# One set of sorted tiles in a fused attention and mixture-of-experts layer, with the last router begun inside the last projection

## The chip, the cores and the metric

The kernel runs on one core of a Trainium2 chip. The core has TensorE (PE; its weight loads are PEld), VectorE (DVE), ScalarE (ACT), GpSimd (POOL) and SyncE (SP), each with a queue of its own that is worked off in order, and 16 DMA engines that carry what SP and POOL issue. The metric is the device time of one execution in microseconds. All arithmetic is in float32.

## The reference

Two batches of 1024 tokens, 256 wide. Modulated layer norm, attention with 16 query heads of 128 and one shared key/value head, an output projection, a second layer norm and a gated residual; then a second modulated norm and a mixture of 8 experts of which each token takes two:

```python
h = _layernorm(x) * (1 + ca) + sa
x = x + ga * attention(h)            # q, k normalised; softmax; @ Wout; layernorm
h = _layernorm(x) * (1 + cb) + sb
x = x + gb * moe(h)

def _moe(x):
    logits = xf @ router_w.T
    topk_vals, topk_idx = jax.lax.top_k(logits, K)        # K = 2
    topk_w = jax.nn.softmax(topk_vals, axis=-1)
    order = jnp.argsort(exp_id)
    x_sorted = xf[order // K]
    y1 = ragged_dot(x_sorted, w1, counts)                 # 256 -> 2 * 176
    y_act = silu(gate) * up
    y2 = ragged_dot(y_act, w2, counts)                    # 176 -> 256
    # back to the tokens' order, times exp_w, the sum of a token's two rows
```

`counts`, how many of the 4096 (token, expert) pairs each expert has, is known only at run time.

## The kernel before

Tokens are held as 16 row tiles of 128 (`NT`), in four blocks of four (`NBLK`, `QT`). The kernel has two stages.

**Attention** (lines 228 to 865) goes block by block. In a block, `attention` walks over 16 heads times 8 key tiles: `s` (L478), exp on ACT (L482), `o` (L493) and the sums on DVE (L498). Other work is hung into these steps by hand with `at(h, j, f)`. `project` (L541) multiplies by Wout, 16 heads for each of the four row tiles (`pr`, L547), and copies each result to `o` with ACT. `Settle` (L570) does what follows for a block: statistics of the output (`of_outputs`, with the rsqrt on POOL at L177 and L178), `residual`, statistics again (`norms`), then for each row tile `logits`: the modulated row on DVE, two transposes (`tp`, L620), a copy on ACT (`rT`), the router's matmuls (`lg`, L625). `weights` finds the two experts of every token (`chosen`) and their weights, with an exp on ACT (L656). `count` numbers the pairs of each expert (two matmuls, then 18 small DVE instructions). For blocks 0 to 2 all this is hung into the attention of the next block. For the last block there is no next block: its router is run in the second stage.

**Experts** (lines 867 to 1066). Sorted tiles of 128 pairs, all of one expert, lie in DRAM (`sorted_x`). There are two separate sets (`SETS`): the pairs of blocks 0 to 2 in set 0, those of the last block in set 1. Each set must have room for any distribution over 8 experts, each with its own unfinished tile: `tiles_for` gives 31 and 15, 46 in all. `bases` turns counts into places (`place_i`) and gives each tile its expert (`at_w1`, `at_w2`). Rows are put in their places by indirect DMAs from POOL (`scatter`, L742), one for each row tile and each of a token's two choices: 24 for set 0, inside the last block's attention, and 8 for set 1. `choose_second` on POOL swaps weight and destination in the rows between the first choices and the second, so it waits for the first choices' scatters.

A loop of 50 steps pipelines the 46 tiles: step `m` does `turn(m)` (two transposes, `xp`, L913), `up(m-1)` (`su`, L928, Silu on ACT L936, product on DVE L938), `gates` and `turn_back(m-3)` (`ap`, L944), and `down(m-4)` (`sy`, L959). DVE evicts with weight and gate into `ysb` (L967, four buffers), and an indirect DMA on POOL puts the rows into `results` (L970), at the place that the row itself carries. Loads of sorted tiles on SP run seven tiles ahead (`PRE`).

Into the same loop are hung, for the last block: `residual` at steps 0 to 3, `norms` at 4, `logits` at 5 to 8, `weights` at 9, `count` at 10, `bases` at 11, and one scatter a step at 12 to 19. Tiles of set 1 begin at step 31.

From step 36 on, `fetch` (L997) loads a row tile's results, three tiles in two steps, as soon as all of set 0 is written, and two steps later `combine` (L1009, L1010) adds the two results and x on DVE and stores (L1011). The last four row tiles are fetched after the loop, when set 1 is complete.

Each engine's queue keeps the planned order: a planner works from priorities in program order and a model of costs; `issue_after` puts an instruction behind a given one on its engine.

Of the kernel before, what the change touches and what calls it, by code (L numbers as in the profile page):

```python
# [28 lines left out]

# [26 lines left out]
def tile_adaln_attention_moe(  # L56
# [36 lines left out]
    def tiles_for(n):  # L93

        return (TOP * n * P + E * (P - 1)) // P

    NM = [tiles_for(t1 - t0) for t0, t1 in SETS]
    MOST = max(t1 - t0 for t0, t1 in SETS)
# [20 lines left out]
    at_w1 = [keep.tile([P, n], I32, name=f"at_w1_{i}") for i, n in enumerate(NM)]  # L119
    at_w2 = [keep.tile([P, n], I32, name=f"at_w2_{i}") for i, n in enumerate(NM)]  # L120

# [38 lines left out]
    counts = const.tile([P, NM[0]], FP, name="counts")  # L160
    minus_half = const.tile([P, QT], FP, name="minus_half")
    nc.vector.memset(minus_half, -0.5)
    rank = const.tile([P, E], FP, name="rank")
# [18 lines left out]
    def statistics(pool, rows, n, name):  # L182
# [11 lines left out]
    sorted_x = [dram.tile([n * P, ROW], FP, name=f"sorted_x{i}") for i, n in enumerate(NM)]  # L194
    results = [
        dram.tile([(TOP * (t1 - t0) + NM[i]) * P, D], FP, name=f"results{i}")
        for i, (t0, t1) in enumerate(SETS)
    ]

    class Scattered:  # L200
# [5 lines left out]

        def add(self, ins):
            ins = ins.ins
            tc.declare_no_dep(ins, group=self.name, reason="each writes rows of its own")
            tc.add_to_no_dep_group(self.name, ins)  # L210
            self.all.append(ins)

        def read(self, ins):
            for s in self.all:
                tc.add_manual_dep(
                    ins.ins,
                    s.name,
                    mybir.DependencyInfo(mybir.DependencyClass.Sync, mybir.DependencyReason.DATA),
                    reason="reads what they wrote",
                )  # L220

    into_x = [Scattered(f"into_x{i}") for i in range(len(SETS))]
    into_results = [Scattered(f"into_results{i}") for i in range(len(SETS))]
# [4 lines left out]
    with ExitStack() as attn:  # L228
# [58 lines left out]
        def tables():  # L287


            with tc.issue_after(latest["pool"]), tc.issue_after(latest["vector"]):  # L290
                for m in range(NM[0]):
                    nc.vector.memset(counts[:, m : m + 1], float(m))
                for e in range(E):
                    nc.vector.memset(rank[:, e : e + 1], float(E - e))
                for t0, t1 in SETS:
                    to = second_to[:, t0:t1]
                    nc.gpsimd.iota(to, [[TOP * P, t1 - t0]], base=0, channel_multiplier=TOP)
                    nc.vector.tensor_copy(rows[:, t0:t1, TO].bitcast(I32), to)
                    nc.vector.tensor_scalar(to, to, 1, None, ALU.add)
                for b in range(B):  # L300
                    nc.vector.memset(rows[:, b * TPB : (b + 1) * TPB, BATCH:], float(b))

        def clear_sorted():
# [3 lines left out]
            for i, (n, to) in enumerate(zip(NM, sorted_x)):  # L307
                by_tile = to.rearrange("(m p) d -> p m d", p=P)
                nc.sync.dma_start(out=by_tile, in_=zero.unsqueeze(1).to_broadcast([P, n, ROW]))
                nobody = work.tile([P, n, 1], I32, tag="z", name=f"nobody_{i}")  # L310
                nc.gpsimd.iota(
                    nobody, [[P, n]], base=TOP * (SETS[i][1] - SETS[i][0]) * P, channel_multiplier=1
                )
                with nc.allow_non_contiguous_dma(reason="one number of each row"):
                    nc.sync.dma_start(out=by_tile[:, :, TO : TO + 1].bitcast(I32), in_=nobody)
# [225 lines left out]
        def project(blk, q, last):  # L541

            o = work.tile([P, QT, D], FP, tag="proj", name=f"proj_{blk}", bufs=1)
# [17 lines left out]
            for i in range(2):  # L561
                heads(ps[i], i, first, HEADS)
                nc.scalar.copy(o[:, i, :], ps[i])
            for i in range(2, QT):
                ps = ps_m.tile([P, D], FP, tag="mm", name=f"pr_{blk}_{i}")
                heads(ps, i, 0, HEADS)
                nc.scalar.copy(o[:, i, :], ps)
            return o

        class Settle:  # L570


            def __init__(self, blk, o):
                self.blk, self.o = blk, o
# [6 lines left out]
            def of_outputs(self):  # L581
                o = self.o
                self.mv, self.rs = statistics(
                    small, [o[:, i, :] for i in range(QT)], QT, f"o{self.blk}"
                )

            def residual(self, i0, i1):
# [4 lines left out]
                for i in range(i0, i1):  # L592
                    nc.vector.tensor_scalar(
                        o[:, i, :], o[:, i, :], self.mv[:, i, 0:1], self.rs[:, i : i + 1],
                        ALU.subtract, ALU.mult,
# [5 lines left out]
            def norms(self):  # L601
                blk = self.blk
                self.mv, self.rs = statistics(
                    self.small, [xs[:, blk * QT + i, :] for i in range(QT)], QT, f"x{blk}"
                )

            def logits(self, i):
# [3 lines left out]
                row = rows[:, t, :D]  # L611
                nc.vector.scalar_tensor_tensor(
                    row, xs[:, t, :], self.mv[:, i, 0:1], one_cb, ALU.subtract, ALU.mult
                )
                nc.vector.scalar_tensor_tensor(
                    row, row, self.rs[:, i : i + 1], sb, ALU.mult, ALU.add
                )
# [3 lines left out]
                rT = self.wide.tile([P, DC, P], FP, tag="h", name=f"rT_{t}")  # L621
                nc.scalar.copy(rT, tp)
                lg = self.psum.tile([P, E], FP, tag=self.tag, name=f"lg_{t}")
# [6 lines left out]
            def weights(self):  # L630
# [25 lines left out]
                nc.scalar.activation(e2, e2, AF.Exp)  # L656
# [5 lines left out]
        filled = [keep.tile([P, E], FP, name=f"filled_{i}") for i in range(len(SETS))]  # L662
        for f in filled:
            nc.vector.memset(f, 0.0)
        end = keep.tile([P, E], FP, name="end")

        filled_in = filled

        def count(blk, filled, work, psum, tag):
# [22 lines left out]
        def bases(i, work):  # L692

            t0, t1 = SETS[i]
            filled = filled_in[i]
            over = work.tile([P, E, MOST], FP, tag="z", name=f"over_{i}")
            nc.vector.tensor_scalar(
                over, counts[:, :MOST].unsqueeze(1).to_broadcast([P, E, MOST]), float(P), None, ALU.mult
            )
            nc.vector.tensor_tensor(  # L700
                over, filled.unsqueeze(2).to_broadcast([P, E, MOST]), over, ALU.is_gt
            )
            nc.vector.tensor_reduce(filled, over, AX.X, ALU.add)
            nc.vector.tensor_copy(end[:, 0:1], filled[:, 0:1])
            for e in range(1, E):
                nc.vector.tensor_tensor(
                    end[:, e : e + 1], end[:, e - 1 : e], filled[:, e : e + 1], ALU.add
                )
            nc.vector.tensor_tensor(filled, end, filled, ALU.subtract)
            nc.vector.tensor_scalar(filled, filled, float(P), None, ALU.mult)  # L710
            n = (t1 - t0) * TOP
            base = work.tile([P, n, E], FP, tag="h", name=f"base_{i}")
            nc.vector.tensor_tensor(
                base,
# [396 lines left out]
```

## Time and profile before

| | |
|---|---|
| time, median of 3 runs | 1354.47 us (1352.80 to 1355.57) |
| the profiled execution | 1353.75 us |
| its span, first to last instruction | 1352.0 us |
| granted TensorE clock, mean | 0.991 |
| TensorE busy | 98% of the span |
| DVE, ACT, POOL busy | 51%, 36%, 17% |
| last attention matmul to last projection matmul | 1186 to 1215.9 us |
| sorted tiles on TensorE | 1216.3 to 1337.9 us |

A group's line on the page reads: line, engine and operation, tiles written and read, number of instructions | busy us, mean ns of one | idle time of the engine just before, and what ended it. A timeline's line reads: start, length, engine, line, operation, tiles, number; in brackets the idle time before it and what released it. A row of the table by stretches reads: from:to, length, then busy us and instructions of PE, PEld, DVE, ACT and POOL, the granted clock, the DMA engines' busy share, and GB/s.

### The profile page before, as it was taken

The numbers are of one execution on the slowest core, as the hardware profiler recorded it, in microseconds if no ns is written. First come the engines' busy times: TensorE is split into PE (matmuls) and PEld (weight loads), VectorE is DVE, ScalarE is ACT, GpSimd is POOL, SyncE is SP. The second block draws the span as 40 slices with busy tenths as digits, with TensorE's granted clock in tenths as the row PEclk, the third lists the DMA queues.
The fourth block names the chain that finished last, engine by engine and source line by source line (L and its number), as shares of the span: only waits on it lengthen the run. The fifth ranks groups of instructions, "written<-read, shape, count | busy, mean of one in ns | idle before, by whom it ended". The sixth has DMA issues, their size and how long they took to land.

```text
span 1352.0 us, 12731 instructions
## 1 busy us (share of the span) xinstructions
PE 1322.1 (98%) x4024; PEld 686.6 (51%) x4024; DVE 685.4 (51%) x1380; ACT 489.4 (36%) x954; POOL 229.1 (17%) x325
## 2 busy tenths in 40 slices
PE   7899999999999999999999999999999999999995
PEld 3444444446644444447444444457444444476774
DVE  6356655544535554542636353544546544437645
ACT  2433344442243433330343333321333333304442
POOL 4200212110100111000100000001000224003633
PEclk9899999999999999999999999999999999999998
DMA  7000000000003410000001200100001013013435
GB/s 245 1 0 19 13 15 18 1 31 32 1 1 121 93 32 0 31 1 32 0 1 32 86 32 0 32 1 32 1 0 32 26 54 103 31 32 119 135 123 194
DMA packets 46322, 59.18 MB, mean 44 GB/s; under 512 B 10672, under 2 KB 32432, under 8 KB 46256
## 3 DMA queue, kind: packets, MB, share of 16 engines
q1 hardware_dynamic: 42512, 48.08, 11.6%
q0 software_dynamic: 3744, 10.29, 2.1%
q8 instruction: 33, 0.54, 0.2%
q14 instruction: 33, 0.27, 0.1%
HBM read 39.69 MB, written 18.66 MB: 43 GB/s over the span
## 4 chain that ended last, share of the span: by engine, by line
PE 93%; DVE 2%; DMA 2%; POOL 2%; issue 1%; ACT 0%; SPq 0%; POOLq 0%; DVEq 0%; ACTq 0%
PE s L478 32%; PE o L493 32%; PE pr L547 8%; PE q L441 8%; PE su L928 3%; PE sy L959 2%; PE qp L455 2%; PE den L507 1%; DMA out_dram<-res 1%; PE kv L384 1%; PE ap L944 1%; PE xp L913 1%; POOL rn_q L178 0%; PE lg L625 0%; DMA wmod_sb<-in_wmod_dram 0%
## 5 line engine op out<-in xcount | busy, mean ns | idle before, releaser
L478 PE MATMUL s<-qT,kT 128*128 128x512 f32 x1024 | 525.5, 595 | 0.1
L493 PE MATMUL o<-p,vs 128*128 128x512 f32 x1024 | 522.7, 593 | 0.0
L482 ACT ACTIVATE p<-s 128x512 f32<-128x512 f32 x512 | 305.6, 597 | 502.4 <-PE s L478 497.3
L498 DVE TENSOR_TENSOR sum<-sum,p 128x512 f32<-128x512 f32 x384 | 264.5, 689 | 180.2 <-ACT p L482 175.5
L493 PEld LDWEIGHTS o<-p,vs 128*128 128x128 f32 x1024 | 193.5, 190 | 233.2 <-issue 232.1
L478 PEld LDWEIGHTS s<-qT,kT 128*128 128x128 f32 x1024 | 187.4, 191 | 206.0 <-issue 204.1
L177 POOL TENSOR_SCALAR rn_q<-rn_q 128x4 f32<-128x4 f32 x64 | 14.0, 219 | 721.1 <-DVE rn_q L344 706.0
L441 PE MATMUL q<-wq_sb,rows 128*128 128x512 f32 x256 | 121.0, 596 | 0.0
L547 PE MATMUL pr<-wout_sb,qT 128*128 128x256 f32 x512 | 112.7, 381 | 0.0
L547 PEld LDWEIGHTS pr<-wout_sb,qT 128*128 128x128 f32 x512 | 96.7, 190 | 18.8 <-issue 4.3
L498 DVE TENSOR_TENSOR sum<-p,p 128x512 f32<-128x512 f32 x64 | 44.2, 691 | 113.4 <-ACT p L482 113.3
L344 DVE TENSOR_REDUCE rn_q<-sq_q 128x4 f32<-128x512 f32 x64 | 43.8, 684 | 84.0 <-ACT sq_q L343 83.9
L178 POOL TENSOR_TENSOR rn_q<-rn_q,minus_half 128x4 f32<-128x4 f32 x64 | 83.3, 1302 | 5.3
L441 PEld LDWEIGHTS q<-wq_sb,rows 128*128 128x128 f32 x256 | 49.1, 192 | 60.5 <-issue 50.5
L347 DVE TENSOR_TENSOR vn_q<-q,rn_q 128x512 f32<-128x512 f32 x64 | 44.2, 690 | 58.2 <-POOL rn_q L178 58.2
L343 ACT ACTIVATE sq_q<-q 128x512 f32<-128x512 f32 x64 | 38.2, 597 | 75.1 <-PE q L441 70.8
L523 DVE TENSOR_TENSOR qT<-qT,wide 128x512 f32<-128x512 f32 x64 | 42.2, 690 | 44.5 <-DMA wide<-spread 44.2
L515 DVE RECIPROCAL rden<-den 128x512 f32<-128x512 f32 x16 | 53.7, 3358 | 20.0 <-PE den L507 20.0
L928 PE MATMUL su<-w_sb,xT 128*128 x184 | 62.9, 462 | 0.2
L970 POOL DMA_INDIRECT results<-ysb,x x46 | 46.4, 1009 | 54.2 <-DVE ysb L967 37.9
L455 PEld LDWEIGHTS qp<-ident,vn_q 128*128 128x128 f32 x256 | 32.3, 143 | 37.3 <-issue 31.2
L959 PE MATMUL sy<-w2s,sactT 128*128 x184 | 47.2, 380 | 0.0
(160 smaller groups left out, 763.4 us busy)
## 6 DMA issues: line engine op xcount, KB each, us to landing
wide<-spread SPq DMA_DIRECT2D x64, 256.0 KB
x<-sorted_x SPq DMA_DIRECT2D x46, 130.0 KB
y<-results SPq DMA_DIRECT2D x16, 256.0 KB
sorted_x<-zero SPq DMA_DIRECT2D x1, 4030.0 KB
w_sb<-in_w_dram SPq DMA_DIRECT2D x2, 1408.0 KB
wout_sb<-in_wout_dram SPq DMA_DIRECT2D x1, 2048.0 KB
out_dram<-res SPq DMA_DIRECT2D x16, 128.0 KB
sorted_x<-zero SPq DMA_DIRECT2D x1, 1950.0 KB
```

What stands on the lines that cost most here:

```text
L178: latest["pool"] = nc.gpsimd.tensor_tensor(out, out, minus_half[:, : out.shape[1]], ALU.pow).ins
L441: nc.tensor.matmul(q.rearrange("p h d -> p (h d)"), hT[:, self.blk * QT + i, c, :], wq_sb[:, c, ts(g, QB)], start=(c == 0), stop=(c == DC ...
L455: nc.tensor.transpose(tp[:, j, :], qn[:, j, :], ident)
L478: nc.tensor.matmul(s, kT[:, ts(b * NJ + j, P)], q.head(h), start=True, stop=True)
L482: nc.scalar.activation(p, s, AF.Exp)
L493: nc.tensor.matmul(outs[h], vs[:, b * NJ + j, :], p, start=(j == 0), stop=(j == NJ - 1))
L498: latest["vector"] = nc.vector.tensor_tensor(sums[h], first, p, ALU.add).ins
L515: nc.vector.reciprocal(rden, den)
L547: nc.tensor.matmul(ps, q.head(h)[:, ts(i, P)], wout_sb[:, h, :], start=(h == 0), stop=(h == HEADS - 1),)
L928: nc.tensor.matmul(u, self.xT[:, c, :], w1_flat[:, c * I2 :][:, bass.ds(at, I2)], start=(c == 0), stop=(c == DC - 1),)
L959: nc.tensor.matmul(y, self.actT[:, c, :], w2_flat[:, c * D :][:, bass.ds(at, D)], start=(c == 0), stop=(c == 1),)
L970: ins = nc.gpsimd.indirect_dma_start(out=results[self.i], out_offset=bass.IndirectOffsetOnAxis(ap=self.x[:, TO : TO + 1].bitcast(I32), axi ...
```

## The change

There is one set. The first three blocks fill `full[e]` whole tiles of each expert `e`, at least 17 together (`FULL`); these come first. Then comes one tile for each expert, its unfinished one (8; with the whole ones at most 32, `ONES`), and the last block's pairs fill these up before they open further tiles; 39 tiles are room for everything (`ALL`). `place_first` gives the first three blocks' pairs their places, `place_second` those of the last block, and both share `places`, `experts`, `tiles_of` and `summed`. `at_w1`, `at_w2`, `sorted_x` and `results` are one tile or tensor each instead of two. Tiles 0 to 16 are loaded after the first 24 scatters, all others after all 32.

`Settle` works on ranges of row tiles: `all_norms(i0, i1)` does both statistics and the residual, `turn` is split from `logits`. In the last block `project` takes steps in `between`: the norms of row tiles 0 to 2, and the router of tiles 0 and 1, are issued among the last projection's matmuls. The rest comes earlier in the expert loop (`late`). The last block's eight scatters go out as two groups of four at steps 9 and 10. The exp of the weights is a power on POOL. The tables of numbers are made by an iota. `ysb` has five buffers. Fetches of the first twelve row tiles begin when tiles 0 to 31 are written, two a step.

```diff
-    NM = [tiles_for(t1 - t0) for t0, t1 in SETS]
+    FULL = -((E * (P - 1) - TOP * SETS[0][1] * P) // P)
+    ONES = TOP * SETS[0][1] + E
+    ALL = (TOP * NT * P + E * (P - 1)) // P
+    PARTS = 3
...
-                for m in range(NM[0]):
-                    nc.vector.memset(counts[:, m : m + 1], float(m))
+                nc.gpsimd.iota(at_w1, [[1, ALL]], base=0, channel_multiplier=0)
+                nc.vector.tensor_copy(counts, at_w1)
...
             for i in range(2, QT):
                 ps = ps_m.tile([P, D], FP, tag="mm", name=f"pr_{blk}_{i}")
-                heads(ps, i, 0, HEADS)
-                nc.scalar.copy(o[:, i, :], ps)
+                for g in range(NG):
+                    heads(ps, i, g * HG, (g + 1) * HG)
+                    if g == NG - 1:
+                        nc.scalar.copy(o[:, i, :], ps)
+                    done(i, g)
...
-                nc.scalar.activation(e2, e2, AF.Exp)
+                nc.gpsimd.tensor_tensor(e2, euler, e2, ALU.pow)
...
+        def place_second(work):
+            more = end[:, 2]
+            tiles_of(limit, work, ALU.is_gt, 0, NT)
+            nc.vector.tensor_scalar(full, full, 1.0, None, ALU.add)
+            nc.vector.tensor_tensor(limit, limit, full, ALU.subtract)
+            nc.vector.tensor_scalar(limit, limit, 0.0, None, ALU.max)
+            summed(more, limit)
+            nc.vector.tensor_tensor(
+                more, more, end[:, 1, E - 1 : E].to_broadcast([P, E]), ALU.add
+            )
+            nc.vector.tensor_tensor(below, end[:, 1], full, ALU.subtract)
+            nc.vector.tensor_tensor(above, more, limit, ALU.subtract)
+            nc.vector.tensor_tensor(above, above, end[:, 1], ALU.subtract)
+            nc.vector.tensor_scalar(limit, full, float(P), None, ALU.mult)
+            for table in (below, above):
+                in_rows(table)
+            places(1, work)
+            experts(FULL, ALL, PARTS, work, "past")
...
+                between = {
+                    (1, NG - 1): [lambda: settle.all_norms(0, 2)],
+                    (2, NG - 1): [lambda: settle.all_norms(2, 3)],
+                    (3, 1): [lambda: settle.turn(0)],
+                    (3, 2): [lambda: settle.logits(0), lambda: settle.turn(1)],
+                    (3, 3): [lambda: settle.logits(1)],
+                }
...
-                load = nc.sync.dma_start(out=self.x, in_=sorted_x[i][ts(m, P), :])
-                into_x[i].read(load)
+                load = nc.sync.dma_start(out=self.x, in_=sorted_x[ts(m, P), :])
+                into_x.read(load, TOP * (SETS[0][1] if m < FULL else NT))
...
-                ysb = mg.tile([P, D], FP, tag="ysb", name=f"ysb_{m}", bufs=4)
+                ysb = mg.tile([P, D], FP, tag="ysb", name=f"ysb_{m}", bufs=5)
...
+        late = {
+            0: [lambda: settle.all_norms(QT - 1, QT)],
+            1: [lambda: settle.turn(QT - 2)],
+            2: [lambda: settle.logits(QT - 2)],
+            5: [lambda: settle.turn(QT - 1)],
+            6: [lambda: settle.logits(QT - 1), settle.weights],
+            8: [lambda: count(NBLK - 1, mg, ps_t, "t"), lambda: place_second(mg)],
+        }
+        SCATTERS = 9
+        for m in range(ALL + LAG):
+            there = ALL if m >= SCATTERS + TOP else FULL
+            while len(tiles) < min(m + 1 + PRE, there):
+                tiles.append(Sorted(len(tiles)))
+            for f in late.get(m, ()):
+                f()
...
+            if SCATTERS <= m < SCATTERS + TOP:
+                k = m - SCATTERS
                 with tc.issue_after(tiles[m - LAG].scattered):
-                    k, t = n // QT, SETS[1][0] + n % QT
-                    if k and t == SETS[1][0]:
+                    if k:
                         choose_second(*SETS[1])
-                    scatter(place_i[:, t, k : k + 1], 1, t)
-
-            n = (m - (NM[0] + LAG)) * 3 // 2
-            for t in range(have, min(n, SETS[0][1])):
+                    for t in range(*SETS[1]):
+                        scatter(place_i[:, t, k : k + 1], t)
+
+            n = (m - (ONES + LAG - 1)) * 2
+            for t in range(have, max(have, min(n, SETS[0][1]))):
```

## The prediction

> **What bounds the kernel now.** I read the page first: shares of the span, the chain that ended last, the costliest groups.
>
> ```profile
> PE 1322.1 (98%) x4024; PEld 686.6 (51%) x4024; DVE 685.4 (51%) x1380; ACT 489.4 (36%) x954; POOL 229.1 (17%) x325
> L928 PE MATMUL su<-w_sb,xT 128*128 x184 | 62.9, 462 | 0.2
> L959 PE MATMUL sy<-w2s,sactT 128*128 x184 | 47.2, 380 | 0.0
> ```
>
> TensorE has work for 98% of the span. su and sy each have 184 matmuls, 4 for each of 46 sorted tiles. The change touches the end of this stretch, so next came the chain in order of time there.
>
> ```profile
> 1257.13 0.86 PE sy L959 x4
> 1258.21 1.19 PE su L928 x4
> 1259.62 0.86 PE sy L959 x4
> ...
> 1304.41 0.87 PE sy L959 x4
> ```
>
> From one sy to the next is 2.49 us: that is one sorted tile, and TensorE sets it. Then the timeline of TensorE, of DVE, of POOL, and of the last 10 us. Columns: start, length, engine and line, what ended the idle time before.
>
> ```profile
> 1216.32 0.88 PE L913 MATMUL xp<-ident,x 128*128 128x128 f32 x6 [0.46 <-ACT proj L567]
> 1222.47 0.44 PE L944 MATMUL ap<-ident,sact 128*128 128x128 f32 x2 [1.17 <-DVE sact L938]
> 1228.40 0.41 PE L620 MATMUL tp<-ident,rows 128*128 128x128 f32 x2 [0.29 <-DVE rows L615]
> 1259.46 1.03 PE L959 MATMUL sy<-w2s,sactT 128*128 x4
> ...
> 1240.76 0.17 DVE L628 COPY ls<-lg 128x8 f32<-128x8 f32 x1 [0.34 <-PE lg L625]
> 1246.05 0.16 DVE L685 TENSOR_TENSOR own<-count,filled 128x8 f32<-128x8 f32 x1
> 1250.42 0.21 DVE L688 TENSOR_REDUCE place<-own 128x8 f32<-128x64 f32 x1
> 1254.15 0.16 DVE L721 TENSOR_TENSOR place_i<-place,first 128x8 int32<-128x8 f32 x1
> ...
> 1262.15 0.96 POOL L742 DMA_INDIRECT sorted_x<-rows,place_i  x1 [0.30 <-issue]
> 1265.41 0.19 POOL L761 COPY rows<-share 128x4 f32<-128x4 f32 x1 [1.03 <-DMA sorted_x<-rows,place_i]
> 1266.13 1.23 POOL L742 DMA_INDIRECT sorted_x<-rows,place_i  x1 [0.41 <-DMA x<-sorted_x]
> ...
> 1308.80 0.32 SPq L997 DMA_DIRECT2D y<-results  x1
> 1342.17 1.75 SPq L997 DMA_DIRECT2D y<-results  x4
> 1344.82 0.43 DVE L1009 TENSOR_TENSOR res<-y 128x256 f32<-128x256 f32 x1 [6.35 <-DMA y<-results]
> ```
>
> The sorted tiles begin at 1216.32. Loop step 16 (counted by its sy, that of tile 12) starts at 1259.46; 29 steps of 2.487 lead to step 45 at 1331.6, the draining steps end TensorE at 1337.94 (+6.36), and 14.06 us more (last scatter, last four fetches from 1342.17, last stores) end the span at 1352.0. The whole is 1259.46 + 72.12 + 6.36 + 14.06.
>
> **The change, part by part.**
>
> *Seven tiles fewer.* 31 + 15 become 39. At 2.487 us: **−17.4**.
>
> *Router of tiles 0 and 1 in the projection, of 2 and 3 early in the loop.* A router tile costs TensorE 0.82 us (a step with one takes 3.30 at 1238.34 to 1241.64, against 2.487), so the projection grows by 1.64. A stall is possible there: turn(0) needs norms that DVE and POOL make in about 9 us from the copy of tile 1, 1202.5, thus by 1212, just when half of the last projection tile is done; 0 to 1.5 us, I take 0. Behind it stand only projection matmuls, and the ACT copy that starts tile 3's norms. The first turn moves from 1216.32 to 1218.0. Before, 43.1 us pass from the first turn to step 16; the matmuls in them are worth 40.1 (17 turns at 0.22, 16 ups at 1.19, 14 turns back at 0.22, 12 downs at 0.87, 4 router tiles, 0.5 of count). The other 3 us are waits such as the 1.17 and 0.29 shown, where ap stands behind the residual of four tiles on DVE; now only one tile's residual (1.25 us and two POOL waits of 1.6) is there. With two router tiles 38.4 remain: step 16 at 1256.5, **−3.0** (0 if as many waits come back).
>
> *Exp to POOL.* It removes two ACT table loads (1.28 us each, near 1242 and 1244), off the path. The power costs what rsqrt's does, 1.0 us on POOL, and only the weight waits for it, not the place.
>
> *Early tables.* 31 memsets become one iota and a copy, the clearing DMA shrinks from 46 to 39 tiles: all beside attention. Placing the first set has some 34 DVE instructions for 21, about 3 us more beside attention, where DVE is half idle: 0, up to 1 us if sums come late for the exps' buffers.
>
> *The places of the last block, and the new wait.* Seventeen full tiles, steps 0 to 16, need nothing of the last block; tile 17's load waits for all 32 scatters. When do these end? Count back from step 16 at 1256.5: step 5 at 1228.0 (periods 2.49, plus 0.6 for the logits and 0.5 for count). The logits of tile 3 follow at 1228.9, their copy ends 1229.9. From copy to chosen experts took 3.0 before: 1232.9. Count stands at the start of step 8, 1234.5, and the first `own` came 1.06 after it: 1235.6. Its 18 DVE instructions took 4.6 (1246.05 to 1250.63): 1240.2. Then 15 instructions took 3.7 with the expert work woven in, 0.245 each; place_second has 31 up to place_i: 7.5, so 1247.7. Four scatters at a period of 1.26: the fourth starts at 1251.8. From a fourth scatter over choose_second to the next scatter took 3.98 (1262.15 to 1266.13): 1255.8; the last starts at 1259.6 and lands 2.5 later, 1262.1. A load of 130 KB takes about 2.7 (a 256 KB fetch from 1342.17 to 1344.82): row tile 17 is there at **1264.8**. Its turn is due at 1256.5 + 0.87 = 1257.4: **+7.4**. Behind it on TensorE stand all later turns and ups; on SP only later loads. On POOL the result scatters of tiles 6 to 9 queue behind the two groups of four; with five ysb buffers, tile 12's eviction waits until about 1264 if they keep the written order, the same stretch, so it is not added. Bounds: 4.2 if TensorE's order lets it finish tiles 12 to 16 meanwhile (5.3 us of work, less about 2 to fill again); 9.1 with the clock, next.
>
> *A rule that speaks against it.* TensorE kept clock 1.00 until 1342 and has 0.51 in the row after, PE having ended at 1337.94:
>
> ```profile
> 1340.00:1342.00 2.00, 0.00 (x0) 0.00 (x0) 0.00 (x0) 0.00 (x0) 0.47 (x1) 1.00 0.24 84
> 1342.00:1344.00 2.00, 0.00 (x0) 0.00 (x0) 0.00 (x0) 0.00 (x0) 0.00 (x0) 0.51 0.37 84
> ```
>
> The Trainium skill, "TensorE: Matmul & The Clock Gate", Part 1, says that about 3.4 us of idleness halve the clock, and that about 3.4 us of work restore it. A 7 us gap would thus cost 1.7 more. By the row alone (about 4 us until it falls) the rest may run warm if some of the gap is filled. I take 7.4, between 4.2 and 9.1.
>
> *The end.* Before, the twelve fetches of the first set start at 1308.80, 4.56 after step 34, and ten tiles hide them. Now tile 31 (step 35) is the last they need and only seven tiles follow. Call the first fetch F = step 35 + 4.56. Combines start after the eviction of step 38, F + 4.4, each 0.88 on DVE (0.42 + 0.42 and a gap); twelve are 10.6, the four evictions and one product woven in 2.4: F + 17.4. Only then can SP, in order, issue the last four fetches; from there to the end took 9.83. So the end is step 35 + 31.8. Without that queue it would be 7.46 + 6.36 + 14.06 = 27.9 after step 35. **+3.9** (0 if DVE and SP keep up, +7 if the bytes decide: 7.2 MB at the 325 GB/s of a full row are 22 us, less than the DVE's time, so nearer 4).
>
> Sum on the span: 1352.0 − 17.4 − 3.0 + 7.4 + 3.9 = 1342.9. The profiled execution took 1353.75, 1.75 around its span: 1344.7. The median of the runs is 0.7 above that: **1345.4 us**.
>
> **Rivals.**
> *No wait* (20%): tile 17 in time. For it: scatters without result scatters between them. Against: the chain of 32 us above, of which each link has a row. 1338.0.
> *The end is hidden* (14%): the wait gives DVE and DMA time and fetches keep pace, 1341.5. Against: DVE needs 1.76 us of combines plus 0.8 per step of 2.49.
> *One table of experts makes a false wait* (5%): at_w1 was two tiles and is one; if a read of an early column waits for the late columns' write, tile 8's up waits until 1250.7, 13 us, which covers the other wait: about 1351. Against: xs and place are written in parts without it.
> *Slower* (9%): the DVE chain. If place_second gets only what the expert work leaves (1.18 us of each 2.49, five instructions), 49 instructions take 24 us instead of 12, tile 17 comes at 1277, the wait is 20: about 1358. It decides from 1274 on, place_i 9 us later than I have it. Against: before, 33 such instructions took 8.3 us in the same mix.
> *As forecast* (52%).
>
> **How the numbers follow.** A measurement of this kernel can tell about 0.2%, 2.7 us, from no change. Faster: 52 + 20 + 14 and half of the 5, less a little for a long wait in the forecast case: 0.87. Same 0.04, slower 0.09. The forecast case by itself is 1341 to 1350 (wait 4.2 to 9.1, end 0 to 7 about 4). The range takes in no-wait below and the false wait above: 1337.5 to 1352; the slower case and a tenth at the low end stay out.
>
> **What would show it.** 156 su matmuls; no wait for rows in the projection; one table load after 1216; the step of tile 12's sy near 1256; place_i near 1248; POOL with four scatters in a row twice; xp waiting for the load of x some 7 us, clock below 1.00 after it; DVE's res waiting for nothing while the last fetches wait behind stores on SP. Wrong if xp never waits, if the span from TensorE's end to the last store stays at 14 us, or if step 16 is later than before.

## The result, and the profile after

| | before | after |
|---|---|---|
| time, median (16 runs each) | 1353.37 us (1351.98 to 1355.57) | 1350.64 us (1348.91 to 1353.15) |
| the profiled execution, and its span | 1353.75, 1352.0 | 1350.09, 1348.4 |
| granted TensorE clock, mean | 0.991 | 0.986 |

The ratio is 0.9981, with an interval of 0.9973 to 0.9989: a gain of 0.19%, at the edge of what can be told from no change, where the forecast had about 9 us. (The same pair measured again, under The experiments, gave 0.9983.) The profiled span fell by 3.6 us. The seven tiles went and took their 17.4 us with them, and 4.5 us more were gained elsewhere; 18.3 us came back in two places.

**The first place: tile 17 waits for its rows, and the clock falls.** First the timeline of the changed kernel: the last place, the POOL scatters that hang on it (the first and the last of the eight), and TensorE's turn of tile 17 between the second products of tiles 12, 13 and 14.

```profile
1244.59 0.15 DVE L753 TENSOR_TENSOR place_i<-place,below 128x8 int32<-128x8 f32 x1
...
1245.39 0.96 POOL L824 DMA_INDIRECT sorted_x<-rows,place_i  x1 [0.30 <-DVE owner L769]
...
1256.94 0.96 POOL L824 DMA_INDIRECT sorted_x<-rows,place_i  x1 [0.30 <-DMA sorted_x<-rows,place_i]
...
1254.95 1.03 PE L1050 MATMUL sy<-w2s,sactT 128*128 x4
1262.19 0.66 PE L1004 MATMUL xp<-ident,x 128*128 128x128 f32 x2 [6.21 <-DMA x<-sorted_x]
1265.96 1.60 PE L1050 MATMUL sy<-w2s,sactT 128*128 x4
...
1269.02 1.03 PE L1050 MATMUL sy<-w2s,sactT 128*128 x4
```

Tile 17's turn was due 0.87 after the start of 1254.95, at 1255.82, and began at 1262.19: 6.4 us late, with the load of its rows as the releaser. From tile 12's `sy` to tile 14's pass 14.07 us, where two steps are 4.97. So 9.10 are lost there, 2.73 more than the wait. The table by stretches of the same kernel (columns as explained with the profile of before) shows where those are:

```profile
1257.00:1259.00 2.00, 0.00 (x0) 0.00 (x0) 0.02 (x1) 0.00 (x0) 1.70 (x2) 1.00 0.38 133
1259.00:1261.00 2.00, 0.00 (x0) 0.00 (x0) 0.00 (x0) 0.00 (x0) 1.39 (x3) 0.82 0.36 75
1261.00:1263.00 2.00, 0.66 (x2) 0.29 (x2) 0.00 (x0) 0.06 (x1) 1.65 (x2) 0.50 0.76 226
1263.00:1265.00 2.00, 1.97 (x4) 1.22 (x5) 0.00 (x0) 0.31 (x1) 0.96 (x1) 0.50 1.04 318
1265.00:1267.00 2.00, 2.00 (x7) 1.46 (x6) 0.34 (x1) 0.69 (x2) 0.00 (x0) 0.50 1.02 362
1267.00:1269.00 2.00, 2.00 (x11) 1.42 (x10) 0.97 (x2) 0.37 (x1) 0.64 (x1) 0.97 0.73 221
```

The third column from the right is the granted clock. It leaves 1.00 inside the second row and is back inside the last one. For 4.9 us after work has begun again, TensorE runs at half its clock: 4 and 7 matmuls in a row, where a warm row has 11 or 12.

**The second place: the end.** The waits of the changed kernel in its last 38 us (engine, line, what it waits for: us in total, times, the longest):

```profile
POOL results L1061 <- DVE ysb L1058: 14.0, 6, 6.3
DVE res L1098 <- DMA y<-results: 6.0, 2, 4.4
DVE res L1098 <- DMA out_dram<-res: 5.3, 1, 5.3
```

The third line is the loss that the change brings: a combine waits 5.3 us for a store, where before the longest such wait was 1.7 (shown further below). The timeline of SP's queue, of DVE and of POOL in that stretch shows how:

```profile
1316.62 6.87 SPq L1086 DMA_DIRECT2D y<-results  x12
1323.80 12.05 SPq L1100 DMA_DIRECT2D out_dram<-res  x11
1337.75 0.33 SPq L1086 DMA_DIRECT2D y<-results  x1
...
1322.52 0.75 DVE L1098 TENSOR_TENSOR res<-y 128x256 f32<-128x256 f32 x2
1323.19 0.75 DVE L1099 TENSOR_TENSOR res<-res,xs 128x256 f32<-128x256 f32 x2
1323.86 0.48 DVE L1058 SCALAR_TENSOR_TENSOR ysb<-sy,x,gb 128x256 f32<-128x256 f32 x1
1329.65 0.91 DVE L1098 TENSOR_TENSOR res<-y 128x256 f32<-128x256 f32 x2 [5.31 <-DMA out_dram<-res]
1330.48 0.76 DVE L1099 TENSOR_TENSOR res<-res,xs 128x256 f32<-128x256 f32 x2
1331.15 0.48 DVE L1058 SCALAR_TENSOR_TENSOR ysb<-sy,x,gb 128x256 f32<-128x256 f32 x1
...
1324.62 0.95 POOL L1061 DMA_INDIRECT results<-ysb,x  x1 [0.51 <-DMA y<-results]
1331.90 1.89 POOL L1061 DMA_INDIRECT results<-ysb,x  x1 [6.33 <-DVE ysb L1058]
1334.10 1.77 POOL L1061 DMA_INDIRECT results<-ysb,x  x1 [0.30 <-DVE res L1098]
```

SP issues twelve fetches of 256 KB in a row and only then, at 1323.80, the first result store. The store's combine was done at 1321.3; it is issued 2.5 us later, and another 5.85 pass until it has landed, among the bytes of the fetches. `res` has four buffers (the pool `my`), so the fifth combine needs the first store landed: 1329.65. Behind that combine in DVE's order stand the evictions of tiles 37 and 38 (1331.15 and the next); behind those, on POOL, their scatters; behind those, on SP, the last four fetches, from 1337.75. TensorE had ended at 1325.6. From there to the end of the span pass 22.8 us, where before they were 14.06.

**The other gains.** Tile 12's `sy` stands at 1254.95 instead of 1259.46. Of these 4.5 us, 1.8 are the attention stage, which ended that much earlier in this execution (its last matmuls, `den`, start at 1186.38 instead of 1188.15). That is chance: in the other profiled executions of the changed kernel and its variants they start between 1186.9 and 1189.9, and in that of the changed kernel measured again at 1188.36. The other 2.7 go with the router's earlier steps; no run below isolates them.

The second profile of the changed kernel has the same terms: tile 12's `sy` 2.5 us nearer to the attention stage than before, tile 17's turn 6.3 late, 2.3 more lost behind it, and 23.4 from TensorE's end to the end of the span.

### The profile page after: what moved, and what is told of

Read it like the earlier page. It is cut to its first block, busy times and chain, and to the rows that moved or that the text cites. A ratio compares the mean times of both kernels' runs of the same rounds, so it can differ in the third digit from the quotient of the medians.

```text
span 1348.4 us, 12430 instructions
## 1 busy us (share of the span) xinstructions
PE 1305.2 (97%) x3940; PEld 674.2 (50%) x3940; DVE 683.3 (51%) x1366; ACT 479.5 (36%) x927; POOL 230.8 (17%) x329
## 4 chain that ended last, share of the span: by engine, by line
PE 90%; DVE 3%; DMA 2%; POOL 2%; issue 1%; ACT 0%; SPq 0%; POOLq 0%; DVEq 0%; ACTq 0%
PE s L478 33%; PE o L493 32%; PE q L441 8%; PE pr L551 8%; PE su L1019 2%; PE qp L455 2%; PE sy L1050 2%; PE den L507 1%; PE kv L384 1%; DMA y<-results 1%; DMA sorted_x<-rows,place_i 1%; PE xp L1004 0%; PE ap L1035 0%; POOL rn_q L181 0%; PE lg L641 0%
## 5 line engine op out<-in xcount | busy, mean ns | idle before, releaser
L1019 PE MATMUL su<-w_sb,xT 128*128 x156 | 54.2, 471 | 0.3 <-issue 0.2
L1061 POOL DMA_INDIRECT results<-ysb,x x39 | 42.2, 1083 | 59.0 <-DVE ysb L1058 46.9
L500 ACT COPY qT<-o 128x512 f32<-128x512 f32 x64 | 37.4, 585 | 22.9 <-PE o L493 22.9
```

Of the source, the lines that this page charges most:

```text
L1019: nc.tensor.matmul(u, self.xT[:, c, :], w1_flat[:, c * I2 :][:, bass.ds(at, I2)], start=(c == 0), stop=(c == DC - 1),)
```

## The experiments

The first batch of four (eight result buffers, both choices in one run, filling alone, scatters sent elsewhere) ran beside a kernel before at 1358.04 us (1356.44 to 1359.41), the other eleven, in three batches, beside one at 1352.38 to 1353.05. Why the kernel before was 5 us slower there is not known. The changed kernel was not in the first batch; it and the one with eight result buffers were measured in the second. The latter agreed within 0.5 us in both, so kernels are compared by their times, not by their ratios. A difference of 1 or 2 us between a run of the first batch and the changed kernel stays uncertain.

### Eight result buffers

```diff
-        my = moe.enter_context(tc.tile_pool(name="my", bufs=4))
+        my = moe.enter_context(tc.tile_pool(name="my", bufs=8))
```

> The changed kernel with eight buffers for the finished rows (res) in place of four. Theory A, DVE stood 5.3 us behind a store because the fifth combine needs the first one's buffer, and the last two evictions stood behind it: that idle time goes, the last result scatter starts some 6 us earlier (after TensorE's end by 7 to 8 us instead of 9.6), and the time falls by 4 to 6 us, to 1344.6 to 1346.6. Rival B, the DMA engines' bytes set the end: DVE waits the same time for fetched rows instead, and the time falls by less than 1.5 us.

> The changed kernel, nothing edited, beside the same runs of the kernel before as the others of this batch: ratio 0.998 again if its small gain is its own; nearer 0.994 if the kernel before is about 4 us slower on this chip, as it was in the first batch of experiments, and the changed one is not.

> Eight result buffers in place of four, once more, now beside the changed kernel itself. Theory A (the fifth combine waits for the store of the first, which stands behind twelve fetches): about 4 to 5 us less than the changed kernel, since the wait of DVE of 5.3 us goes. Theory B (the bytes of the fetches set the end): within 1.5 us of the changed kernel.

Eight buffers: 1346.10 us in the first batch. In the second: the changed kernel 1351.41 (1348.10 to 1353.70; ratio 0.9983, 0.9975 to 0.9991), with eight buffers 1345.60 (1345.00 to 1346.53; ratio 0.9949, 0.9933 to 0.9966). That is 5.8 us for one number. Theory A holds. In both profiled executions of the second batch TensorE ends at the same point, 1327.3; the span goes on for 23.4 us with four buffers and for 16.0 with eight. In their waits near the end, the first line is that of four buffers, the second that of eight:

```profile
DVE res L1098 <- DMA out_dram<-res: 6.1, 1, 6.1
DVE res L1098 <- DMA out_dram<-res: 1.5, 1, 1.5
```

The table by stretches shows DVE standing still with four buffers (first row, from the changed kernel's first profile) and at work with eight (the other two):

```profile
1326.00:1328.00 2.00, 0.00 (x0) 0.00 (x0) 0.00 (x0) 0.00 (x0) 0.00 (x0) 1.00 1.05 407
1326.00:1328.00 2.00, 1.10 (x4) 0.68 (x4) 2.00 (x8) 0.00 (x0) 1.71 (x1) 1.00 1.04 399
1328.00:1330.00 2.00, 0.00 (x0) 0.00 (x0) 1.48 (x5) 0.00 (x0) 1.61 (x2) 1.00 1.05 401
```

The DMA engines are full with either number of buffers (407 and 399 GB/s from 1326 to 1328), so the bytes alone do not set the end.

### The stores issued by ScalarE

```diff
-            nc.sync.dma_start(out=ot[:, t, :], in_=res)
+            nc.scalar.dma_start(out=ot[:, t, :], in_=res)
```

> The result stores are issued by ScalarE instead of SyncE; four result buffers as in the changed kernel. If what delays the store of tile 0 is SyncE's order (it stands behind twelve fetches): it leaves right after the first combine, about 1320, the fifth combine waits 2 us at most and the end comes 3 to 5 us earlier. If the delay is the transfer itself (the DMA engines full of fetches until 1330): the fifth combine still waits 4 us or more, and the time is within 1.5 us of the changed kernel. A loss is possible where ScalarE's copies stand behind a store that waits for its combine.

1349.95 us (1347.91 to 1351.35), 1.5 below the changed kernel, between the two expectations. Timeline of ScalarE's queue and of ScalarE, then the fifth combine on DVE:

```profile
1325.16 0.86 ACTq L1100 DMA_DIRECT2D out_dram<-res  x2
1326.12 0.32 ACT L1027 ACTIVATE sg<-su 128x176 f32<-128x176 f32 x1 [6.11 <-DMA y<-results]
...
1330.14 0.76 DVE L1098 TENSOR_TENSOR res<-y 128x256 f32<-128x256 f32 x2 [0.78 <-DMA out_dram<-res]
```

The first store leaves at 1325.16, no earlier than from SP, and lands 5 us later. Its combine was done at 1321.9 and ScalarE had been idle since 1320.0, so SP's order is not all that holds the store's issue; the profile names a fetch as what ScalarE waited for, and why is not shown. The fifth combine waits only 0.8 us because DVE is late itself: the store stands in ScalarE's order, the Silu behind it is 6.1 us late, and TensorE ends at 1332.7 instead of 1327.3, its last tiles at clock 0.50. The expectation named this danger, not its size. What part of the 8.3 us from the combine's end to the store's landing each cause could give back alone stays open; that more buffers free DVE from both is shown above.

### Matmuls that fill the gap

```diff
+            if m == FULL:
+                ps = ps_y.tile([P, D], FP, tag="y", name="fill")
+                for _ in range(13):
+                    nc.tensor.matmul(ps, ident, gb[:, 0, :], start=True, stop=True)
             if m < ALL:
                 tiles[m].turn()
```

> The changed kernel with 13 matmuls of 128x256 that nobody reads, 5.6 us of work, ahead of tile 17's turn: they fill the idle time and nothing else. Theory A, the idle time halves the granted clock and the first steps after it cost 2.7 us more: clock 1.00 all through the sorted tiles, step of tile 14's sy 7.1 us instead of 7.1 + 2.7 behind tile 17's turn less its own, and the time falls by 2 to 2.7 us (1348 to 1348.6). Rival B, the slow steps after the wait come from late rows and buffers, not from the clock: no change, or up to 1 us slower.

> Eight result buffers, and 13 matmuls that nobody reads ahead of the turn of tile 17, so that TensorE does not cool while it waits for the rows. If both losses are separate they add: e1's gain (4 to 5 us) and the clock's 2.7 us less what the filling matmuls delay (0 to 1), together 6 to 7 us below the changed kernel, about 1 to 2.5 below e1b. If the slack of the end swallows one of them, it equals e1b within 1 us.

Alone: 1348.50 us (1348.06 to 1348.69), 2 to 3 below the changed kernel, which ran in other batches. With eight result buffers: 1341.70 (1340.80 to 1342.38; ratio 0.9916, 0.9899 to 0.9933), 3.9 below eight buffers alone, where the profiled spans differ by 2.7. That is more than expected. The two losses are separate: each cure alone gives 5.8 and 2 to 3 us, both together 9.7. The rows of the second kernel where the clock had been at half:

```profile
1261.00:1263.00 2.00, 2.00 (x11) 1.71 (x9) 0.00 (x0) 0.00 (x0) 1.42 (x2) 1.00 0.29 91
1263.00:1265.00 2.00, 1.13 (x5) 0.50 (x4) 0.00 (x0) 0.37 (x1) 1.67 (x2) 1.00 0.90 261
1265.00:1267.00 2.00, 2.00 (x11) 1.46 (x10) 0.34 (x1) 0.65 (x2) 1.22 (x2) 1.00 0.99 280
```

The clock stays at 1.00, and from tile 12's `sy` to tile 14's 6.9 us are lost instead of 9.7 with eight buffers alone.

### No wait for the rows

```diff
-                into_x.read(load, TOP * (SETS[0][1] if m < FULL else NT))
+                into_x.read(load, TOP * SETS[0][1])
```

In the first of two such kernels the eight scatters go to another tensor, in the second they are left out (and it has eight result buffers). Both leave out the expert outputs of the last block.

> The changed kernel with the last block's eight scatters sent to another tensor of the same size, and all loads of sorted tiles waiting for the first 24 scatters alone. It leaves out the last block's expert outputs: the last four fetches read the results of other tokens. All other work and all transfers are there. Theory A: the wait at tile 17 and the clock's fall after it are gone, TensorE ends 9.1 us earlier, and, if the end behind it is as long as before, the time falls by 9 us to 1341.5. Rival B, the end is set by the fetches' transfers: they start 9.1 us earlier too, so the same. Rival C, DVE or DMA work piled up in the wait comes back: less than 6 us.

> Eight result buffers, and the eight row scatters of the last block are left out; every load of a sorted tile waits for the first 24 only, and the last four fetches read the results of other tokens, so the output lacks the last block's experts. It shows what the wait of tile 17 and the scatters on GpSimd cost together. If the wait and the cold clock are a plain loss: 6.5 + 2.7 us below the kernel with eight result buffers alone, 1336.5. If the end, full of transfers, takes part of it back: 1338 to 1342. If the stall of all engines seen near 1266 with the scatters sent elsewhere has another cause than the eight scatters, it is here too.

Without the scatters: 1336.43 us (1335.66 to 1339.15), 9.2 below eight buffers alone and within 0.1 of the first of the expected cases. So the wait, the cold clock and whatever else the eight scatters cost are a plain loss, once the result buffers don't hold the end. With the scatters sent elsewhere: 1348.23, of four executions three at 1347.5 to 1348.7 and the profiled one at 1352.51. That is 2 to 3 us below the changed kernel, the third of the expected cases (less than 6). With four result buffers its end still waits 5.0 us for a store. The profiled execution has no wait for tile 17's rows, but ScalarE, DVE and TensorE stand still for about 5 us near 1266 to 1271, with no releaser that the profile can name. The kernel without scatters has nothing of the kind.

### Both choices of the last block in one run of eight scatters

The second choices get a copy of the rows of their own (made on ScalarE and GpSimd in steps 6 to 8, not shown), so that GpSimd need not wait between the two groups:

```diff
-                    if k:
-                        choose_second(*SETS[1])
                     for t in range(*SETS[1]):
-                        scatter(place_i[:, t, k : k + 1], t)
+                        row = again[:, t - SETS[1][0], :] if k else rows[:, t, :]
+                        scatter(place_i[:, t, k : k + 1], t, row)
```

> The changed kernel with a second copy of the last block's rows, made on ACT, that carries the second choice's weight and place, so that the second group of four scatters waits for nothing. Theory A, TensorE stands at tile 17 because the eighth scatter is late: it goes out 2.7 us earlier (no landing, no result scatter between the groups), tile 17's turn comes 2.7 us earlier, the idle time there is 3.5 us instead of 6.2, the clock stays up longer, and the time falls by 2.7 to 5.4 us (1345.2 to 1347.9). Rival B, the end is set by the transfers whatever comes before: less than 1 us.

1351.88 us (1351.00 to 1353.53): no gain. Tile 17's turn no longer waits for its rows, but other waits stand earlier, again with no named releaser:

```profile
1254.74 0.37 ACT L1006 COPY xT<-xp 128x256 f32<-128x256 f32 x1 [4.73 <-remote]
1257.90 0.34 DVE L1029 TENSOR_TENSOR sact<-sg,su 128x176 f32<-128x176 f32 x1 [5.06 <-issue]
1260.15 2.08 PE L1050 MATMUL sy<-w2s,sactT 128*128 x4 [3.23 <-issue]
```

During these, POOL issues eleven scatters, one each 1.27 us. A run of ten goes with the stall of the kernel with the scatters sent elsewhere. But a run alone does not make the stall: the fastest kernel below has ten in a row from 1251.32 to 1263.75, and TensorE works beside them. What holds the engines is not settled.

### The router's steps

First attempt to undo the router's move: nothing in the projection, turns at steps 3 to 6. Second: with the step numbers of the kernel before.

```diff
-                between = {
-                    (1, NG - 1): [lambda: settle.all_norms(0, 2)],
...
+            0: [lambda: settle.all_norms(0, QT)],
+            5: [lambda: settle.turn(0)],
...
+            10: [lambda: count(NBLK - 1, mg, ps_t, "t"), lambda: place_second(mg)],
...
-        SCATTERS = 9
+        SCATTERS = 11
```

> The router's move is undone: all four tiles of the last block go through it in loop steps 0 to 7, as in the kernel before, nothing inside the projection. The forecast's step: tile 12's sy comes 3.0 us later. The rows of tile 17 hang on the logits of tile 3, which come one step later, so the wait for them does not shrink by as much. Together 1 to 4 us slower than the changed kernel; 0 if all of it goes into the wait.

> The router's move is undone with the steps of the kernel before: turns in loop steps 5 to 8, the weights in 9, the places in 10, the scatters from step 11. The forecast's term: tile 12's sy 3.0 us later than in the changed kernel. The places come two steps later (5 us) besides, so the wait for tile 17 grows by about 5: 6 to 9 us slower than the changed kernel, about 1358.

1364.58 us (ratio 1.0095, 1.0078 to 1.0112) and 1362.25 (1.0072, 1.0055 to 1.0089): some 13.5 and 11 us slower than the changed kernel, more than expected. The first puts the turn of row tile 0 at a step whose rows aren't there (TensorE stands 8.1 us for them). The second takes 47.2 us from the first turn to tile 12's `sy`, against 43.1 in the kernel before, with TensorE idle 2.1 us before `ap`, 1.2 before `tp` and 1.8 before `count`, where before it was 1.2, 0.3 and nothing. `all_norms` does the residuals of four row tiles in one piece here, where before they came one a step; that this makes the first two is likely and not tested. So neither isolates the 3.0 us. But the second shows the other half: the places are ready at 1258.2, and tile 17's turn waits 11.0 us, until 1275.80.

Then the opposite, one step earlier, in the changed kernel alone and with both cures (eight buffers; 8 filling matmuls):

```diff
-            5: [lambda: settle.turn(QT - 1)],
-            6: [lambda: settle.logits(QT - 1), settle.weights],
-            8: [lambda: count(NBLK - 1, mg, ps_t, "t"), lambda: place_second(mg)],
+            4: [lambda: settle.turn(QT - 1)],
+            5: [lambda: settle.logits(QT - 1), settle.weights],
+            7: [lambda: count(NBLK - 1, mg, ps_t, "t"), lambda: place_second(mg)],
         }
-        SCATTERS = 9
+        SCATTERS = 8
```

> In the changed kernel alone, the last router tile turns in step 4 instead of 5, the weights, the places and the scatters follow one step earlier each. If the wait hangs on the chain router, places, scatters: it falls from 6.3 by about 2.5 to 3.8 us, and with a shorter gap the clock may stay up: 2.5 to 5 us below the changed kernel, 1345.5 to 1348. If it hangs on GpSimd's queue or on the rows of the router being late in step 4 (TensorE waits there): within 1 us.

> One step earlier, with eight result buffers and 8 filling matmuls (3.4 us): the wait shrinks by 2.5 against the kernel with buffers and 13 filling matmuls (1341.7): 1339.3. If the end swallows it: 1341.

Alone: 1347.69 us (1345.53 to 1351.57), some 3 to 3.7 below the two measurements of the changed kernel, as the first expected case has it. The wait is 4.4 us and not 6.2:

```profile
1263.55 0.41 PE L1004 MATMUL xp<-ident,x 128*128 128x128 f32 x2 [4.43 <-DMA x<-sorted_x]
```

The clock fell here too (0.73 in the row 1263 to 1265, 0.50 in the next) and cost 2.2 us more. With both cures: **1340.17 us** (1339.15 to 1341.35; ratio 0.9910, 0.9894 to 0.9927). That is 1.5 below the kernel without the earlier step, between the two expectations, and the fastest measured here of the kernels that compute everything, ahead of both given ones. From tile 12's `sy` to tile 14's it loses 4.5 us.

From the places to the turn of tile 17 pass 17.6 us in the changed kernel, 16.6 and 17.6 in the two attempts to undo the router's move, 18.1 with it one step earlier, and 17.2 in the best kernel. The wait hangs on the router's chain, of which the scatters are the fixed second half.

### The exponential back on ScalarE

```diff
-                nc.gpsimd.tensor_tensor(e2, euler, e2, ALU.pow)
+                nc.scalar.activation(e2, e2, AF.Exp)
```

> The weight's exponential goes back to ScalarE (with its two table loads), the rest as changed. The forecast counted this part as nothing: within 1 us of the changed kernel. If the table loads hold ScalarE's copy xT or sactT: 1 to 2.5 us slower.

1350.64 us (1348.50 to 1352.14): within 0.8 us of both measurements of the changed kernel, as expected.

### Combines later, last fetches first

Twelve result buffers and the filling matmuls, and:

```diff
-            while fetched and fetched[0][0] <= m - 2:
+            while fetched and fetched[0][0] <= m - 4:
...
+        last4 = [(t, fetch(t)) for t in range(*SETS[1])]
         for _, t, y in fetched:
             combine(t, y)
-        fetched = [(t, fetch(t)) for t in range(*SETS[1])]
+        fetched = last4
```

> Twelve result buffers, the 13 filling matmuls, combines two steps later (behind more of the last evictions), and the last four fetches issued before the stores of the combines that are left. If the last scatters wait behind combines in VectorE's order (tile 38's scatter ends near 1329 with eight buffers and filling): the last fetches come 2 to 3 us earlier and the end with them, 1339 to 1340. If the transfers fill the time (the DMA share is about 1.0 from 1318 to 1332): within 1 us of 1341.7.

1345.89 us (1343.97 to 1346.14), 4.2 slower than with eight buffers and filling matmuls: both expectations fail. The evictions do come earlier, but the last scatter does not end (timeline of POOL, then two lines of DVE's):

```profile
1325.20 1.90 POOL L1061 DMA_INDIRECT results<-ysb,x  x1 [0.51 <-DVE ysb L1058]
1327.40 5.45 POOL L1061 DMA_INDIRECT results<-ysb,x  x1 [0.30 <-DVE res L1098]
...
1327.91 0.75 DVE L1098 TENSOR_TENSOR res<-y 128x256 f32<-128x256 f32 x2
...
1331.27 0.75 DVE L1099 TENSOR_TENSOR res<-res,xs 128x256 f32<-128x256 f32 x2
```

DVE runs additions of two operands without a gap from 1327.91 to 1332.02. The scatter that otherwise takes 0.96 us lasts until 1332.85, 0.83 us after the last addition, and the last fetches leave at 1334.44 instead of 1331.65. The DMA engines were not what it waited for; their share in that stretch is the last but one number here:

```profile
1330.00:1332.00 2.00, 0.00 (x0) 0.00 (x0) 2.00 (x7) 0.00 (x0) 2.00 (x1) 0.50 0.14 46
```

## Why the prediction was wrong

The forecast summed to 1342.9 us on the span; it was 1348.4. By its own steps:

| step | forecast | measured |
|---|---|---|
| seven tiles at 2.487 | −17.4 | −17.4 (156 `su` matmuls, same period) |
| router earlier: tile 12's `sy` | −3.0 | −2.7 (4.5 earlier, less 1.8 of the attention stage; not isolated) |
| wait for tile 17's rows | +7.4 | +6.4 |
| clock behind the wait | 0 taken, 1.7 by the rule | +2.7 |
| the end | +3.9 | +9.2 |
| attention stage | 0 | −1.8 (chance) |
| sum | −9.1 | −3.6 |

**"The end" is the step that failed.** Its words were "Combines start after the eviction of step 38, F + 4.4, each 0.88 on DVE": the twelve were taken to run at DVE's pace, with the stores held to matter only for SP's order behind them. In their place, the fifth combine waits for the first store, because a combine needs a buffer as well as its operands, and the buffer comes free only when the store has landed behind twelve fetches. The forecast's own sign for this stretch, DVE's `res` waiting for nothing, is the one that failed: it waited 5.3 us. The kernel before had a trace of it, which the forecast did not read: the first store left after seven fetches, and one combine waited 1.7 us for a store, while TensorE had tiles left to hide it. Its SP queue (behind the first fetch, at 1308.80) and its waits near the end say so:

```profile
1309.69 0.92 SPq L997 DMA_DIRECT2D y<-results  x2
...
1311.95 5.78 SPq L997 DMA_DIRECT2D y<-results  x4
1317.82 0.44 SPq L1011 DMA_DIRECT2D out_dram<-res  x1
...
DVE res L1009 <- DMA out_dram<-res: 1.7, 1, 1.7
```

In the changed kernel all twelve fetches go first and TensorE has two tiles left. From tile 31's `sy` to the end the forecast had 31.8 us; it was 37.1. With eight buffers, from TensorE's end to the end of the span, it is 16.0 us, where the forecast's working gives 18.0 (31.8, less 7.46 and 6.36), and 14.06 before. So with nearly all of that wait gone the term is about 2, below the forecast's 3.9; its upper bound of 7 was drawn around another cause, bytes, and the 9.2 lie outside it.

**The clock was mis-sized.** The wait was right in place and nearly in size. The forecast took 0 for the clock behind it, since "the rest may run warm if some of the gap is filled", but nothing in the planned order put TensorE work into the gap. Its own row ("about 4 us until it falls") already had the clock fall inside a gap of 7 us; it still set the cost of coming back at 0. The rule of the Trainium skill ("TensorE: Matmul & The Clock Gate", Part 1) was nearer: an estimate of 1.7 by its figure, 2.7 here, since the clock took 4.9 us of work to return, not 3.4. That wait and clock together meet the forecast's upper bound of 9.1 exactly is luck: the wait came 1.0 short and the clock 1.0 over.

**Right, or nearly:** the places at 1244.7 instead of 1247.7; GpSimd's eight scatters and `choose_second`, with one result scatter between the groups that was not in the count; from the last scatter's start to the turn 5.25 us (forecast 5.2); the power at 1.05 us and without effect (also by the experiment). POOL held back result scatters in the same stretch, as said, those of tiles 7 to 11 instead of 6 to 9. The signs named for a failure were right in kind: the span from TensorE's end to the last store did change from 14 us, though to 22.8.

**Rivals.** No wait: refuted by the 6.21 in the trace. The end hidden: refuted, it was the largest loss. The false wait of one expert table: the 156 `su` matmuls have 0.3 us of idle time before them in all. The slow DVE chain: the places came early. What happened was the forecast's own case with two of its terms too small. Its range (1337.5 to 1352) holds the time only thanks to the room left at the top for the false wait, which did not come; the case's own upper end of 1350 does not hold it.

## What to carry to other kernels

When a change bunches transfers that were spread (here twelve fetches issued before the first store), follow each buffer to the moment it comes free, not only each operand to the moment it arrives; a pool of four cost one hidden wait of 1.7 us at three fetches in two steps, and 5.8 us of the time here. When a change moves a dependency closer, price the gap and the clock behind it as two terms, and remember that a handful of unread matmuls can buy back the second. An engine that issues a store for another's data takes over that engine's waits.

## What the runs showed of the hardware

**The clock.** Nine profiled executions have a gap of 4.4 to 11.0 us before tile 17's turn. After TensorE's last matmul before it the granted clock fell 3.6 to 5.3 us later (4.3 in the changed kernel, 3.6 in its second profile), and it came back 3.0 to 6.0 us after the first matmul behind the gap (4.9 and 4.3). These are worked out from the share of 1.00 in the rows of the tables by stretches in which the clock changes. In the kernel with the router one step earlier the first matmul came at 1263.55 and the clock fell about 1263.9, after work had begun. Where the kernel is the changed one around the gap, the slow matmuls cost 2.2 us behind a gap of 4.4 and 2.3 to 3.1 behind gaps of 5.2 to 6.7.

**Scatters beside VectorE's two-operand additions.** A scatter took 0.95 to 1.2 us among the steps of the expert loop, 0.95 to 1.9 beside combines, and 5.45 where combines ran without a gap; that one ended 0.83 us after the last addition, with the DMA engines at 0.14. The Trainium skill ("SBUF — State Buffer", "SBUF: two separate sides") says that VectorE with two SBUF inputs can hold a port pair that it shares with GpSimd, but only against a GpSimd instruction that reads SBUF; where it tells of GpSimd kept from writing the descriptors of its transfers, it names VectorE's two-port modes alone. The durations here would fit such a lock by additions; that it was this port is not shown.

**Stalls with no releaser.** In two kernels with eleven and ten scatters in a row, one each 1.27 us, ScalarE, VectorE and TensorE lost 2 to 5 us with no releaser in the profile. A third kernel with ten in a row lost nothing. Not settled.
